# Norm factors computed in four column groups and spread by DMA, in the local layers and in sink attention

## The chip, the cores and the metric

The kernel runs on one core of one Trainium2 chip. The metric is the device time of one execution in microseconds, here the median over runs of the same kernel. A core has a tensor engine (PE, whose weight loads are shown apart as PEld), a vector engine (DVE), a scalar engine (ACT), GpSimd (POOL) and a queue engine (SP) that issues most transfers. They run side by side and wait for each other through semaphores. Operands lie in an on-chip memory of 128 partitions; products land in PSUM, which has eight banks of 128 x 512 fp32.

## The reference

The program is a network of sixteen residual blocks over x of 16 x 256 tokens with 128 channels, all in fp32. Each block computes `x = x + block(layernorm(x))`. Two blocks matter here.

The local block (it occurs twice, each time as two layers one after the other): half of the channels are shifted by one token, then projected to queries, keys and values of 8 heads of 64; these are normalized, rotated, and attended in windows of 64 tokens that see themselves and the window before. After the output projection and a residual sum, half of the channels are shifted again, a layer norm with gain `lg` and bias `lb` follows, and a gated feed-forward part with 341 hidden channels.

The sink-attention block (it occurs once): an RMS norm, grouped attention with 16 query heads and 4 key heads, interleaved rotary positions, a band of 128 tokens, and one sink logit per head:

```
combined = jnp.concatenate([scores, sink], axis=-1)
probs = jax.nn.softmax(combined, axis=-1)[..., :-1]
out = jnp.einsum('buqk,bkuh->bquh', probs, v)
```

The kernel computes in this block both the outer layer norm with its inner RMS norm (two factors from one variance), and after the attention the RMS norm that the mixture of experts starts from (one factor).

What is changed is how one number per token, `1 / sqrt(mean of squares + eps)`, comes about and reaches all 128 partitions.

## The kernel before

Activations lie transposed: channels on partitions, tokens along the free dimension. The 4096 tokens are cut into `NCH = 8` chunks of `CH = 512`, or `NTILE = 32` tiles of `P = 128`. A norm has three steps. `centre_step` multiplies a chunk by `cent` (identity minus 1/128) on PE, which subtracts the mean over channels; ACT copies the result out and POOL (or ACT) squares it into `nsq`. `spread_step` multiplies `nsq` by `mean`, a 128 x 128 matrix filled with 1/128. The product holds the same variance on each of the 128 partitions, so it is summed and spread at once; ACT turns it into the factor `nrs` in two passes over 128 x 512 (Ln with eps added, then Exp scaled by -0.5), or four passes where two factors are wanted. The third step multiplies the chunk by the factor on DVE. Constants (`cent`, `mean`, the identity) lie in the tile `ct`, which is the name that the profile shows.

The stages concerned run under a schedule written out by hand: each engine executes its instructions in the order in which the loops record them.

`local_attend` loops over m from -9 to 37. One step of m scores and weighs one unit of work (a 256-token stretch and half of the heads), turns and rotates one tile of queries and keys, and projects a tile that is needed five steps later. Within a step the order is: scores, weighing, output projection every fourth step, transposes and values (`turn`), exponentials, `rotate`, the inverse of the sums and the division (`rd`, `ot`), `unit`, then `chunk_steps`, then `project`. The norm steps stand in `chunk_steps`: for the first layer of a pair the norm of x of chunk c at m = 4c - 9, 4c - 8, 4c - 7 (chunks 0 to 4 were normalized by the stage before, `led`), and in both layers the norm ahead of the feed-forward part (`norm_of_half`) at m = 4c + 6 to 4c + 9, for chunks 0 to 6. PSUM is shared as three banks `w` (projections, transposes, norms), four `s` (scores) and one `o`.

`window_attention` is the sink attention. It loops over n; each n scores one of 128 units, and each odd n weighs two. Even n carry the rest: `prepare` (the rotary projections of a chunk's half: key and first query group, two groups, one group, none, in four even n one after the other), `out`, `before(c, 0..2)` for the norm before attention of chunk c at n = 16c - 14, -12, -10, and `after(c, 0..2)` for the norm after it at n = 16c + 24, +26, +28. Scores, projections and norms share four `s` banks. A matrix product can only start when the last reader of the bank it gets is done, and which bank it gets is settled when the program is built.

Transfers: weights of a coming stage are loaded on SP by `ahead`, three DMAs each, which wait until the stage that used the buffer is done. During the first local layer, SP also issues 66 transfers (`fill_rooms`) that initialize tables in device memory for the later expert stages: `rows` in 64 transfers of 520 KB and two small ones. No transfer takes part in any norm.

Of the kernel before, what the change touches and what calls it, by code (L numbers as in the profile page):

```python
# [11 lines left out]
F32, BF16, I32 = mybir.dt.float32, mybir.dt.bfloat16, mybir.dt.int32  # L12
SP = mybir.EngineType.SP
AF = mybir.ActivationFunctionType
# [3 lines left out]
P = 128  # L18
B, T, C = 16, 256, 128
NT = B * T  # L20
CH = 512
NCH = NT // CH
# [1627 lines left out]
class Fast(Net):  # L1650
# [120 lines left out]
            self.gt(sq, dst, dst, ALU.mult)  # L1771
        return sq

    def spread_step(self, pool, sq, bank, eps="eps5", twice=False):


        pv = self.bank(bank)
        self.mm(pv, self.k["mean"], sq)
        out = []
        for n in range(2 if twice else 1):  # L1780
            rs = pool.tile([P, CH], F32, tag=f"nrs{n}", name="nrs", bufs=2)
            if n:
                self.act(rs, pv, AF.Ln, scale=1.0 + 1e-5, bias=self.k["eps10"])
            else:
                self.act(rs, pv, AF.Ln, bias=self.k[eps])
            out.append(rs)
        for rs in out:
            self.act(rs, rs, AF.Exp, scale=-0.5)
        return out if twice else out[0]

    def norm_steps(self, pool, src, dst, bank, g=None, b=None, eps="eps5", copy=None, square=False):


        held = {}

        def centre():
            held[0] = self.centre_step(pool, src, dst, bank, copy, square)

        def spread():
            held[1] = self.spread_step(pool, held[0], bank, eps)  # L1800

        def scale():
            if g is None:
                self.tt(dst, dst, held[1], ALU.mult)
            else:
                self.stt(dst, dst, g, held[1], ALU.mult, ALU.mult)
                self.ts(dst, dst, b, ALU.add)

        return [centre, spread, scale]

    def norm_x_step(self, pool, c, i, bank="ps", copy=None):

        if c in self.led:
            return
        if i == 0:
            s = self.chunk(c)
            self.norms[c] = self.norm_steps(pool, self.x[:, s], self.ha[:, s], bank, copy=copy)
        self.norms[c][i]()

    def slots(self, n, *steps, last=(), every=1):  # L1820
# [1339 lines left out]
    def window_attention(self, w, h, n1, ns2):  # L3160


        nc = self.nc
        with ExitStack() as st:
            p1 = self.stage(st, "w1", 1)
# [27 lines left out]
            def later(slot, f, *args):  # L3193
                due.setdefault(slot, []).append((f, args))
# [24 lines left out]
            def score(n):  # L3219
                c, side, b, it, jt = units[n]  # L3220
                i0, j0 = b * T + it * P, b * T + jt * P
                q, k = qs[2 * c + side], ks[2 * c + side]
                pt = p2.tile([P, 2, 4, P], F32, tag="pt", name="pt", bufs=6)
                ps = [self.bank("s"), self.bank("s")]
                for half in range(2):
                    rows = slice(64 * half, 64 * half + 64)
                    self.mm(ps[half].rearrange("p (h t) -> p h t", h=4), k[rows, j0 : j0 + P], q[rows, :, i0 : i0 + P])
                for half in range(2):
                    self.act(pt[:, half].rearrange("p h t -> p (h t)"), ps[half], AF.Exp)
                pts[n] = pt  # L3230
# [53 lines left out]
            def out(i):  # L3284
                c, side = divmod(i, 2)
                pz = self.bank("s")
                ot = ots.pop(i)
                for g in range(4):
                    at = (4 * side + g) * C
                    self.mm(pz, w["Wof"][:, at : at + C], ot[:, g], start=g == 0, stop=g == 3)  # L3290
                hs = h[:, self.chunk(c)]
                if side:
                    self.tt(hs, hs, pz, ALU.add)
                else:
                    self.stt(hs, pz, w["bo"], hs, ALU.add, ALU.add)

            held = {}

            def before(c, i):

                s = self.chunk(c)
                if i == 0:
                    held["sq"] = self.centre_step(p1, self.x[:, s], h[:, s], "s", square=True)
                elif i == 1:
                    held["rs"] = self.spread_step(p1, held["sq"], "s", twice=True)
                else:
                    r1, r2 = held["rs"]
                    self.stt(n1[:, s], h[:, s], w["ns1"], r2, ALU.mult, ALU.mult)
                    self.tt(h[:, s], h[:, s], r1, ALU.mult)

            def after(c, i):

                s = self.chunk(c)
                if i == 0:
                    held["sq"] = p1.tile([P, CH], F32, tag="nsq", name="nsq", bufs=2)
                    self.act(held["sq"], h[:, s], AF.Square)
                elif i == 1:
                    held["rs"] = self.spread_step(p1, held["sq"], "s")
                else:
                    self.stt(n1[:, s], h[:, s], ns2, held["rs"], ALU.mult, ALU.mult)  # L3320

            with self.share(s=4, o=4), self.tc.manual_schedule():
                self.logs()
                for n in range(-14, len(units) + 16):
                    if 0 <= n < len(units):
                        score(n)
                        later(n + 1, masked, n)
                    for f, args in (*due.pop(n, []), *due.pop(("last", n), [])):
                        f(*args)
                    if n % 2:  # L3330
                        for i in (n - 3, n - 2):
                            if 0 <= i < len(units):
                                weigh(i, n)
                        continue
                    i, step = divmod(n + 8, 8)
                    if 0 <= i < 2 * NCH:
                        prepare(i, step // 2, n)
                    i, rest = divmod(n - 14, 8)
                    if rest == 0 and 0 <= i < 2 * NCH:
                        out(i)  # L3340
                    c, u = divmod(n + 14, 16)
                    if u in (0, 2, 4) and c < NCH:
                        before(c, u // 2)
                    c, u = divmod(n - 24, 16)
                    if u in (0, 2, 4) and 0 <= c < NCH:
                        after(c, u // 2)

    def local_begin(self):
        pass
# [8 lines left out]
    def local_attend(self, w, z, hs, last):  # L3358
# [5 lines left out]
        nc = self.nc  # L3364
        with ExitStack() as st:
            p = self.stage(st, "l1", 1)
# [15 lines left out]
            made, rot, qkt, val, weights, sums, outs, steps, spare = {}, {}, {}, {}, {}, {}, {}, {}, []  # L3382
# [141 lines left out]
            def chunk_steps(m):  # L3524

                def due(slot):
                    c, rest = divmod(m - slot, 4)
                    return c if rest == 0 and 0 <= c < NCH else None

                if not last:  # L3530
                    for i in range(3):
                        if (c := due(i - 9)) is not None:
                            self.norm_x_step(p, c, i, "w")
                for slot in (-6, 5):
                    if (c := due(slot)) is not None:
                        self.shift(hs[:, self.chunk(c)], z[:, self.chunk(c)])

                for i in range(4):
                    if (c := due(6 + i)) is not None and c < NCH - 1:
                        if i == 0:  # L3540
                            steps[1] = self.norm_of_half(p, "w", w, hs[:, self.chunk(c)])
                        steps[1][i]()

            with self.share(w=3, s=4, o=1), self.tc.manual_schedule():
                self.logs()
                for m in range(-9, NTILE + 6):
# [4 lines left out]
                    c, rest = divmod(m - 5, 4)  # L3551
# [14 lines left out]
                    if within(m + 5, NTILE):  # L3566
                        project(m + 5)

    def norm_of_half(self, pool, bank, w, s):

        held = {}

        def centre():
            held[0] = self.centre_step(pool, s, s, bank)

        def spread():
            held[1] = self.spread_step(pool, held[0], bank)

        return [
            centre, spread, lambda: self.stt(s, s, w["lg"], held[1], ALU.mult, ALU.mult),  # L3580
            lambda: self.act(s, s, AF.Identity, bias=w["lb"]),
        ]
# [263 lines left out]
```

## Time and profile before

| | us |
|---|---|
| median of 3 runs (range) | 4256.13 (4253.08 to 4257.88) |
| profiled execution, its own time | 4251.58 |
| span of the profiled execution | 4249.8 |
| PE busy, over the span | 3860.8 (91%) |
| DVE busy | 2557.6 (60%) |
| ACT busy | 2327.2 (55%) |
| POOL busy | 1852.0 (44%) |
| `nrs` from PSUM on ACT, 128x512, mean of 208 | 0.683 |
| `nrs` in place on ACT, 128x512, mean of 208 | 0.629 |

Attention of the four local layers runs from about 115, 485, 1125 and 1490 us on, some 280 us each; sink attention runs from about 2915 to 3388 us. The busy time of an engine is the union of its instructions. Line L504 is a matrix product, L508 a transpose, L528 an activation, L531 and L543 are DVE's two- and three-operand operations and L534 is POOL's: they are helpers, so groups are told apart by the names of the tiles. An operand written `ps<-nsq,ct` means that a PSUM tile is written from the tiles nsq and ct. An fp32 product appears as two records, one for each of its two passes.

### The profile page before, as it was taken

The page shows a single profiled execution, that of the slowest core. Times are in us where ns is not written, and L with a number is a line of the kernel's source. Part 1 is how long each engine was busy: PE and PEld are TensorE (multiplying, and loading weights), DVE is VectorE, ACT ScalarE, POOL GpSimd, SP SyncE. Part 2 cuts the span into 40 slices and gives each one's busy share as a digit, 9 for nine tenths or more (in the row PEclk, how much of TensorE's full clock was granted, in tenths as well). Part 3 has the DMA queues.
Part 4 walks back from the last instruction along what each step waited for, and adds up shares of the span by engine and source line. Part 5 has one row for each costly group of instructions (what it writes and reads, how often), then busy time and mean ns, then how long its engine had stood idle before and what let it go on. Part 6 is the DMA issues. An engine that isn't in the chain of part 4 may idle for free. (4 is left out here: it accounts for less than half of the span.)

```text
span 4249.8 us, 73853 instructions
## 1 busy us (share of the span) xinstructions
PE 3860.8 (91%) x28998; PEld 2207.7 (52%) x28998; DVE 2557.6 (60%) x4503; ACT 2327.2 (55%) x4741; POOL 1852.0 (44%) x1632
## 2 busy tenths in 40 slices
PE   7999999998899999995989979888999999899878
PEld 3555466464465456553965459643444344455333
DVE  4775577364477477555336643565788687486474
ACT  6665466554766456553447634444555455774432
POOL 4664365232565166316433334454555455311251
PEclk9999999988999999997999979999999999999989
DMA  1800000000000000002930049100000000000000
GB/s 61 343 1 1 11 1 1 20 1 1 20 1 1 1 4 2 1 1 83 330 125 12 17 137 316 61 19 16 1 1 1 3 1 1 16 2 18 6 0 21
DMA packets 78404, 176.43 MB, mean 42 GB/s; under 512 B 12606, under 2 KB 39108, under 8 KB 77920
## 3 DMA queue, kind: packets, MB, share of 16 engines
q1 hardware_dynamic: 65568, 148.40, 10.1%
q0 software_dynamic: 9120, 18.51, 1.2%
q8 instruction: 231, 3.78, 0.4%
q10 hardware_dynamic: 3360, 4.72, 0.3%
q14 instruction: 125, 1.02, 0.1%
HBM read 118.28 MB, written 54.20 MB: 41 GB/s over the span
## 5 line engine op out<-in xcount | busy, mean ns | idle before, releaser
L528 ACT ACTIVATE pt<-ps 128x512 f32<-128x512 f32 x640 | 340.0, 600 | 327.7 <-PE ps L504 326.4
L504 PE MATMUL ps<-hb,w 128*128 128x512 f32 (+1 forms) x960 | 458.7, 611 | 6.9 <-issue 3.3
L504 PE MATMUL ps<-w,hb 128*128 128x512 f32 (+2 forms) x896 | 403.4, 571 | 27.9 <-DVE t L531 20.9
L534 POOL TENSOR_TENSOR t<-t,t 128x512 f32<-128x512 f32 x256 | 319.3, 1268 | 160.8 <-DVE t L531 101.2
L531 DVE TENSOR_TENSOR t<-ps,tab 128x512 f32<-128x512 f32 x512 | 317.5, 681 | 83.8 <-ACT sq L528 80.3
L534 POOL TENSOR_TENSOR t<-t,ss 128x1024 f32<-128x1024 f32 x128 | 243.5, 1903 | 218.9 <-ACT ss L528 217.6
L504 PEld LDWEIGHTS ps<-hb,w 128*128 128x128 f32 (+1 forms) x960 | 178.0, 190 | 263.7 <-issue 224.3
L528 ACT ACTIVATE qkt<-ps 128x512 f32<-128x512 f32 x256 | 140.5, 595 | 309.0 <-PE ps L508 308.4
L531 DVE TENSOR_TENSOR u<-u,ps 128x384 f32<-128x384 f32 (+1 forms) x206 | 121.8, 595 | 287.9 <-PE ps L508 182.9
L531 DVE TENSOR_TENSOR ot<-ps,rd 128x512 f32<-128x512 f32 (+2 forms) x224 | 143.2, 639 | 232.0 <-ACT rd L528 232.0
L534 POOL TENSOR_TENSOR nsq<-ha 128x512 f32<-128x512 f32 x112 | 122.9, 1097 | 320.4 <-ACT ha L528 308.6
L504 PEld LDWEIGHTS ps<-w,hb 128*128 128x128 f32 x896 | 155.5, 192 | 185.4 <-issue 113.6
L534 POOL TENSOR_TENSOR both<-pt 128x1024 f32<-128x1024 f32 x64 | 151.2, 2362 | 200.0 <-DVE pt L531 164.3
L504 PE MATMUL ps<-nsq,ct 128*128 128x512 f32 x368 | 201.0, 629 | 36.0 <-POOL nsq L534 32.1
L504 PE MATMUL ps<-ot,w 128*128 128x512 f32 x448 | 213.6, 611 | 16.8 <-DVE ot L531 9.0
L504 PE MATMUL ps<-xt,w 128*128 128x128 f32 x1704 | 221.0, 280 | 1.5 <-ACT xt L528 1.5
L2199 POOL DMA_INDIRECT back<-y,x x142 | 138.9, 978 | 184.2 <-ACT y L528 90.4
L504 PE MATMUL ps<-u,w 128*128 128x512 f32 (+1 forms) x448 | 215.4, 605 | 3.4 <-POOL u L534 3.4
L528 ACT ACTIVATE u<-ps,w 128x512 f32<-128x512 f32 x160 | 107.8, 685 | 183.8 <-PE ps L504 181.3
L504 PEld LDWEIGHTS ps<-xt,w 128*128 128x128 f32 x1704 | 204.8, 194 | 2.9 <-ACT xt L528 2.9
L528 ACT ACTIVATE nrs<-ps,ct 128x512 f32<-128x512 f32 x208 | 139.8, 683 | 101.8 <-PE ps L504 95.9
L3743 POOL DMA_INDIRECT rows<-out,idx x128 | 125.8, 982 | 155.1 <-ACT out L528 105.7
(362 smaller groups left out, 8937.9 us busy)
## 6 DMA issues: line engine op xcount, KB each, us to landing
w<-in_moe_x SPq DMA_DIRECT2D x142, 533.0 KB
rows<-t SPq DMA_DIRECT2D x64, 520.0 KB
x<-rows SPq DMA_DIRECT2D x142, 65.0 KB
w<-in_local_f SPq DMA_DIRECT2D x8, 659.5 KB
y<-back ACTq DMA_DIRECT2D x16, 256.0 KB
y<-back SPq DMA_DIRECT2D x16, 256.0 KB
w<-in_local_f SPq DMA_DIRECT2D x4, 658.5 KB
back<-y,x POOLq DMA_INDIRECT x142
```

The source lines that it names most:

```text
L504: self.nc.tensor.matmul(out, lhsT, rhs, start=start, stop=stop)
L528: self.nc.scalar.activation(out, in_, func, **kw)
L531: self.nc.vector.tensor_tensor(out, a, b, op)
L534: self.nc.gpsimd.tensor_tensor(out, a, b, op)
L2199: nc.gpsimd.indirect_dma_start(views[i], bass.IndirectOffsetOnAxis(ap=x[:, C : C + 1].bitcast(I32), axis=0), y, None, bounds_check=2 * NT ...
L3743: nc.gpsimd.indirect_dma_start(views[(c * 2 + k) * 4 + t], bass.IndirectOffsetOnAxis(ap=idx[:, k, t : t + 1], axis=0), out[:, k, t], None,)
```

## The change

A `compact` form of `spread_step` is added. It multiplies the four groups of 128 tokens of a chunk by only 32 columns of `mean`, and puts the result of group r onto partitions 32r to 32r + 31. One PSUM tile of 128 x 128 then holds the variances of all 512 tokens, each on 32 equal rows. ACT's passes run over 128 x 128 elements (two factors: their Exp together over 128 x 256) into a new tile `nrow`. Four DMAs for each factor, issued on SP, write `nrs`: each reads the 32 equal rows of a group four times and fills 128 partitions and 128 columns. The step that scales waits for these DMAs.

The form is used for the norms of x in `local_attend`, for `norm_of_half` on chunks 0 to 6, for the norm before sink attention on chunks 1 to 7, and for the norm after it on chunks 0 to 6. The other norms keep the old form. In sink attention the steps of the loop also move: for chunks 1 to 7, `before` centres and spreads two n earlier (16c - 16 and 16c - 14) and scales at 16c - 10 as it did; `after` scales two n later for chunks 0 to 6 (16c + 30).

```diff
+    def compact_spread(self, pool, sq, bank, eps, twice):
+        nc = self.nc
+        pv = self.bank(bank)
+        for r in range(4):
+            nc.tensor.matmul(
+                pv[32 * r : 32 * r + 32, :P], self.k["mean"][:, :32], sq[:, r * P : r * P + P],
+                start=True, stop=True, skip_group_check=True,
+            )
+        many = 2 if twice else 1
+        rows = pool.tile([P, many, P], F32, tag="nrow", name="nrow", bufs=2)
+        self.act(rows[:, 0], pv[:, :P], AF.Ln, bias=self.k[eps])
+        if twice:
+            self.act(rows[:, 1], pv[:, :P], AF.Ln, scale=1.0 + 1e-5, bias=self.k["eps10"])
+        flat = rows.rearrange("p n t -> p (n t)")
+        self.act(flat, flat, AF.Exp, scale=-0.5)
+        out = []
+        for n in range(many):
+            rs = pool.tile([P, CH], F32, tag=f"nrs{n}", name="nrs", bufs=2)
+            for r in range(4):
+                nc.sync.dma_start(rs[:, r * P : r * P + P], rows[32 * r : 32 * r + 32, n][:, None].broadcast_to([32, 4, P]))
+            out.append(rs)
+        return out if twice else out[0]
...
-                    held["rs"] = self.spread_step(p1, held["sq"], "s", twice=True)
+                    held["rs"] = self.spread_step(p1, held["sq"], "s", twice=True, compact=c > 0)
...
-                    held["rs"] = self.spread_step(p1, held["sq"], "s")
+                    held["rs"] = self.spread_step(p1, held["sq"], "s", compact=c < NCH - 1)
...
-                    c, u = divmod(n + 14, 16)
-                    if u in (0, 2, 4) and c < NCH:
-                        before(c, u // 2)
+                    c, u = divmod(n + 16, 16)
+                    if c == 0 and u in (2, 4, 6):
+                        before(c, u // 2 - 1)
+                    if u in (0, 2, 6) and 0 < c < NCH:
+                        before(c, (u + 1) // 3)
                     c, u = divmod(n - 24, 16)
-                    if u in (0, 2, 4) and 0 <= c < NCH:
-                        after(c, u // 2)
+                    if u in (0, 2, 6 if c < NCH - 1 else 4) and 0 <= c < NCH:
+                        after(c, (u + 1) // 3 + (u == 4))
...
-                            self.norm_x_step(p, c, i, "w")
+                            self.norm_x_step(p, c, i, "w", compact=True)
...
-                        steps[1] = self.norm_of_half(p, "w", w, hs[:, self.chunk(c)])
+                        steps[1] = self.norm_of_half(p, "w", w, hs[:, self.chunk(c)], compact=True)
```

More of the change, by code (lines that the diff above doesn't have):

```diff
@@ L1772, in centre_step, with spread_step @@
         return sq
-    def spread_step(self, pool, sq, bank, eps="eps5", twice=False):
+    def spread_step(self, pool, sq, bank, eps="eps5", twice=False, compact=False):
+        if compact:
+            return self.compact_spread(pool, sq, bank, eps, twice)
         pv = self.bank(bank)
@@ L1789, in spread_step, with norm_steps @@
         return out if twice else out[0]
-    def norm_steps(self, pool, src, dst, bank, g=None, b=None, eps="eps5", copy=None, square=False):
+    def compact_spread(self, pool, sq, bank, eps, twice):
[20 more added lines that the diff above has]
+        return out if twice else out[0]
+    def norm_steps(self, pool, src, dst, bank, g=None, b=None, eps="eps5", copy=None, square=False, compact=False):
         held = {}
@@ L1799, in spread @@
         def spread():
-            held[1] = self.spread_step(pool, held[0], bank, eps)
+            held[1] = self.spread_step(pool, held[0], bank, eps, compact=compact)
         def scale():
@@ L1809, in norm_steps, with norm_x_step @@
         return [centre, spread, scale]
-    def norm_x_step(self, pool, c, i, bank="ps", copy=None):
+    def norm_x_step(self, pool, c, i, bank="ps", copy=None, compact=False):
         if c in self.led:
@@ L1816, in norm_x_step @@
             s = self.chunk(c)
-            self.norms[c] = self.norm_steps(pool, self.x[:, s], self.ha[:, s], bank, copy=copy)
+            self.norms[c] = self.norm_steps(pool, self.x[:, s], self.ha[:, s], bank, copy=copy, compact=compact)
         self.norms[c][i]()
@@ L3567, in local_attend, with norm_of_half @@
                         project(m + 5)
-    def norm_of_half(self, pool, bank, w, s):
+    def norm_of_half(self, pool, bank, w, s, compact=False):
         held = {}
@@ L3576, in spread @@
         def spread():
-            held[1] = self.spread_step(pool, held[0], bank)
+            held[1] = self.spread_step(pool, held[0], bank, compact=compact)
         return [
```

## The prediction

> **What bounds the kernel now.** I read the two-tenths rows of the page for the stages, then busy time by stretch, then the order of instructions inside one step, since the change lives in two stages that a mean over the span hides. Busy time by stretch (first columns: stretch, its us, then PE, PEld, DVE, ACT, POOL busy; then granted clock); a first local layer, a second one, and the sink-attention stage:
>
> ```profile
> 140.00:380.00 240.00, 232.40 (x2310) 144.53 (x2309) 178.09 (x262) 156.68 (x413) 146.97 (x129) 1.00 0.28 111
> 500.00:745.00 245.00, 239.72 (x2468) 151.99 (x2467) 177.49 (x269) 159.35 (x427) 148.22 (x129) 1.00 0.01 2
> ...
> 2940.00:3380.00 440.00, 437.23 (x3428) 179.25 (x3426) 349.56 (x550) 231.44 (x509) 245.37 (x141) 1.00 0.00 1
> ```
>
> PE is busy 97 to 99% at full clock, DVE 73 to 79%, ACT 53 to 65%. A busy PE need not be a full one, so I looked at its instructions in one step of a second local layer (start, us, engine, line, operands; each fp32 product is recorded as two passes):
>
> ```profile
> 593.34 1.02 PE L504 MATMUL ps<-w,hb 128*128 128x512 f32 x2
> ...
> 594.20 1.02 PE L504 MATMUL ps<-nsq,ct 128*128 128x512 f32 x2
> ...
> 595.06 1.88 PE L504 MATMUL ps<-w,hb 128*128 128x512 f32 x4
> ...
> 595.94 0.40 ACT L528 ACTIVATE rd<-ps 128x256 f32<-128x256 f32 x1
> ...
> 596.77 0.39 PE L504 MATMUL ps<-masked,identb 128*128 128x128 bf16 x4
> ```
>
> Starts follow each other every 0.43 us per pass: there is no hole. The spread's product, nsq by ct, holds PE for 595.06 - 594.20 = 0.86 us. So what is worth money is PE time, and only where PE does not then wait for someone else.
>
> **What the Trainium skill says.** "TensorEngine Tiling (Array Packing)", Theoretical Speedup and Key Properties: products with at most 32 stationary columns can run four at once, up to 4 times faster, and a change of tiling mode drains the array. The trace agrees on both, below. "DMA: Bandwidth & Descriptors", Anatomy of one DMA: about 2 us fixed per DMA (fitted for GpSimd's queue); here the final output DMAs show less. The same page, Queues, rings and completion order: an engine consumes descriptors in ring order, so a small DMA behind large ones on SP waits for them; the trace of before has no such pair to show it.
>
> **The change, part by part.** The built program has 48 compact spreads: 10, 7, 10, 7 in the four local layers and 14 in sink attention, 7 of these with two factors. That is 55 factors, so 220 DMAs of 64 KB on SP.
>
> PE. The weighing uses the same form, four 32-column products side by side over 128 columns:
>
> ```profile
> 208.12 0.40 PE L3487 MATMUL ps<-pu,v 128*32 128x128 f32 x8
> ...
> 208.34 0.51 PE L3487 MATMUL ps<-pt,v 128*32 128x192 f32 x8
> ```
> ```profile
> 592.08 0.40 PE L3487 MATMUL ps<-pu,ct 128*32 128x128 f32 x8
> ...
> 592.41 1.09 PE L508 MATMUL ps<-ct,t 128*128 128x128 f32 x8
> ```
>
> A group of four takes 0.22 us (208.34 - 208.12), and 0.33 when a full-array product follows: leaving the mode costs 0.11. Entering it from full mode I take as 0.09, from the change of full to row mode in the sink stage (0.95 below against 0.86). Sum 0.42, saving 0.86 - 0.42 = 0.44 us. Bounds: 0.33 with a free entry (saves 0.53), 0.60 if the entry loses two more passes' setup (saves 0.26).
>
> ACT. Two activations of 128x512 (683 and 629 ns by their groups) become two of 128x128; the nearest row, pu from PSUM, is 279 ns. That gives 0.75 us per spread. ACT is off the path, so nothing, except that squares behind it start sooner.
>
> Where the 0.44 us goes. In second layers it survives only while PE does not overtake ACT: the masks after the projections need the bank that ACT reads as rd, done at 595.94 + 0.40 = 596.34. PE comes at 596.77, so 0.43 us of room plus the first two masks: just covered. Of the 34 local spreads, 6 (chunks 1 to 3 of both first layers) stand in a step where the next norm's centring shares the banks:
>
> ```profile
> 233.14 0.58 ACT L528 ACTIVATE ha<-ps 128x512 f32<-128x512 f32 x1
> ...
> 233.77 1.13 PE L504 MATMUL ps<-w,hb 128*128 128x512 f32 x2 [0.74 <-ACT ha L528]
> ```
>
> PE already waits 0.74 us there for ACT's copy, which does not move: these 6 gain 0. The last compact chunk of each layer stands in the tail, where PE waits on DVE and ACT 0.62 us just after it: 4 gain 0. Left: 24 x 0.44 = 10.6 us.
>
> Sink attention. A spread there costs 0.95 us, and 0.53 is offered. But all 14 now stand behind two rotary projections:
>
> ```profile
> 3023.37 1.98 PE L504 MATMUL ps<-hb,w 128*128 128x512 f32 x4
> ...
> 3025.19 1.02 PE L504 MATMUL ps<-nsq,ct 128*128 128x512 f32 x2
> 3025.20 0.74 DVE L543 SCALAR_TENSOR_TENSOR q<-ps,w 128x512 f32<-128x512 f32 x1
> ...
> 3026.14 1.13 PE L504 MATMUL ps<-q,k 64*128 64x512 f32 x4
> ```
>
> The scores at 3026.14 need four banks' oldest: the first projection's, free when DVE ends at 3025.94. PE ready at 3025.61 would wait. In 7 (before attention) the gain is some 0.15; in the other 7 the built program gives the scores the spread's own bank, free after ACT's logarithm at about 3025.28 + 0.20 + 0.28 + 0.28, so 0.05. Together 1.4 us. Moving the centring two slots ahead takes 0.86 from one step and puts it in another, where DVE frees the first bank at 2991.72 and PE would come at 2991.92: nothing, and up to 0.3 x 7 if that cover is gone. Scaling after attention moves two slots later; nobody in the stage waits for it.
>
> The DMAs. Three loads take 1.29 us to issue, so 0.48 apart. The second output DMA (256 KB) was issued by 4234.22 and released DVE at 4235.65, so 64 KB lands in at most 1.4 us. Four factors: 3 x 0.48 + 1.4 = 2.9 us; eight: 4.8. The consumer comes 7.2 us after the Exp in second layers (564.03 to 571.27), 3.5 in the tail (409.5 to 413.0), and over 13 in sink attention after the move. Hidden, cover lost only beyond 7.2 us (tail 3.5); then DVE stands still with its rotary products queued behind, and PE waits for these. The bytes, 14 MB over some 1400 us, are no load. On SP these DMAs are put behind a wait once: before layer 1's first spread stands the zero-fill.
>
> ```profile
> 111.76 0.33 SPq L2129 DMA_DIRECT2D back<-t  x1
> 113.03 0.82 SPq L2128 DMA_DIRECT2D rows<-t  x2
> 114.99 1.50 SPq L615 DMA_DIRECT2D w<-in_local_f  x3
> 116.53 84.83 SPq L2128 DMA_DIRECT2D rows<-t  x64
> ```
>
> SP is free at 201.36, but the last fill packets run to 208.1, and the consumer wants its factor at 207.4: some 1.5 us late on DVE, I take 1 on PE, once. Weight loads pushed behind the spreads (performer at 480.65 before) waited for their buffer until then anyway: nothing.
>
> Sum: -10.6 - 1.4 + 1.0 = -11.0 us. The profiled execution took 4251.58 us, 4.55 under the median of the runs shown, so 4240.6 on its scale, 4245 on the median's.
>
> **Rivals.** (a) Full saving: everything PE no longer does is gained, 34 x 0.44 + 14 x 0.53 = 22.4 us, 4234. For it: PE busy shares. Against: the bank waits above. (b) It does nothing: entry and exit drains and the ACT cover eat it, -4 us or less, 4252 to 4256. For it: cover of 0.43 against 0.44; against: the drains measured. (c) Slower: the factors land late. If each DMA of a factor began only when the one before had landed, four would take 4 x (0.48 + 1.4) = 7.5 us or, at the skill's 2 us, 9.9, beyond the 7.2 from which it decides; the in-order DVE would lose up to 2.7 us in each of 24 spreads that PE feels, less 11: up to +50, likelier some +15, 4271. Against: three loads issued 0.48 apart without waiting for each other.
>
> **How the numbers follow.** My sum 0.60, (a) 0.16, (b) 0.13, (c) 0.11. The likeliest case alone spans 4238 to 4250 (24 x 0.26 to 0.53, first stall 0 to 2 us). The range reaches over (a) and most of (b): 4233 to 4256. A change under 0.2% (8.5 us) can hardly be told from none here; a part of my own case falls inside it, and (b) does: faster 0.71, same 0.18, slower 0.11.
>
> **What would show it.** nsq by ct at 128x128 in groups 0.42 us before the next product; PE busy in the local stretches down by 0.44 us per spread but a wait of some 0.3 us on DVE or ACT before the scores after each spread in sink attention; the wait on ACT's ha copy grown from 0.74 to about 1.2; factors landing about 3 us after the Exp; DVE idle on a DMA once, near 207. Chunk pitch 34.35 to about 33.9 us in second layers, 56.65 to about 56.4 in sink attention. Wrong if DVE's scaling rows show DMA waits in every chunk, or if the pitch in sink attention falls by a whole 1 us.

## The result, and the profile after

The changed kernel takes 4249.18 us (median of 15 runs, 4243.12 to 4250.94) where the kernel before takes 4256.13 us in the same comparison (15 runs, 4251.52 to 4260.14): a ratio of 0.9983, 95% interval 0.9975 to 0.9991. That is 6.95 us, or between 3.8 and 10.6. The gain is real and lies just inside the 0.2% bound that the prediction set for "can hardly be told from none". The forecast was 4245, its range 4233 to 4256.

The profiled execution took 4250.35 us, with a span of 4248.6. This is only 1.2 us less than the span before, so the two traces can't be compared end to end. Between them lie differences in stages that the change doesn't touch: 1.66 us before the first local layer has even begun its windows, 3.4 us where the expert stage waits for its first gathered rows, and dips of PE's granted clock that cost some 1.6 us each and fall elsewhere in each execution (the 30 us behind the last tile of the first local layer had 0.94 of the full clock in the trace of before and 1.00 in this one). I therefore compare stage by stage: for one VectorE instruction that occurs once per tile in the local layers (the reduction of squares, `ss<-sq`) and one per chunk in sink attention (the sum into `ha`), the starts in the two traces give the length of each chunk. Undisturbed chunks agree within 0.02 us from run to run, so a tenth of a microsecond can be read.

| stretch | before | after | difference |
|---|---|---|---|
| first local layer, chunk with the first spread | 34.13 | 37.66 | +3.53 |
| first layers, chunk with two spreads | 37.95 | 37.38 | -0.57 |
| second layers, chunk with one spread | 34.35 | 33.70 to 33.76 | -0.65 to -0.59 |
| sink attention, chunk | 56.65 | 56.61 | -0.04 |
| sink attention and its run-in, 2823 to 3384 us of before | 560.5 | 559.8 | -0.7 |

Nineteen chunks of the local layers became shorter by 0.56 to 0.65 us, one of them by only 0.31, together 11.0 us. One more became 3.5 us longer. With sink attention the sum is -11.0 + 3.5 - 0.7 = -8.2 us, inside the interval of the measurement.

Busy time by stretch of the changed kernel, for the three stretches shown in the prediction (columns: stretch, its us, then PE, PEld, DVE, ACT and POOL busy; then granted clock, DMA share, GB/s):

```profile
140.00:380.00 240.00, 229.47 (x2366) 143.15 (x2365) 175.53 (x260) 150.49 (x409) 146.11 (x127) 0.99 0.33 122
...
500.00:745.00 245.00, 239.84 (x2508) 152.26 (x2508) 178.02 (x270) 156.35 (x429) 148.63 (x129) 0.99 0.03 8
...
2940.00:3380.00 440.00, 436.91 (x3515) 180.25 (x3512) 348.75 (x549) 218.36 (x499) 245.38 (x141) 1.00 0.06 14
```

ACT lost 13 us in sink attention and PE's busy share hardly moved: in a fixed window, shorter work is followed at once by more work. In the first stretch PE idles 10.5 us where it idled 7.6. That is the stall below. Busy shares alone would have told almost nothing here.

One step of a second local layer, in order of time, the step that the prediction showed at 593 to 597:

```profile
593.09 1.02 PE L504 MATMUL ps<-w,hb 128*128 128x512 f32 x2
...
594.04 0.42 PE L1798 MATMUL ps<-nsq,ct 128*32 128x128 f32 x8
...
594.39 1.98 PE L504 MATMUL ps<-w,hb 128*128 128x512 f32 x4
...
596.22 0.39 PE L504 MATMUL ps<-masked,identb 128*128 128x128 bf16 x4
...
596.79 0.35 ACT L528 ACTIVATE nrow<-ps,ct 128x128 f32<-128x128 f32 x1
...
597.17 0.31 ACT L528 ACTIVATE nrow<-nrow 128x128 f32<-128x128 f32 x1
```

The four products with eight passes take 594.39 - 594.04 = 0.36 us (by the unrounded starts). The product ahead of them occupies PE 0.52 us in place of 0.43, which is the entry into the mode. Over both, PE spends 0.88 us where it spent 1.29: it saves 0.41. ACT's two instructions take 0.35 and 0.31 us in place of 0.67 and 0.63: it saves 0.64.

The first spread of the first local layer, the same view:

```profile
198.66 5.25 SPq L2154 DMA_DIRECT2D rows<-t  x4
...
200.82 0.31 ACT L528 ACTIVATE nrow<-nrow 128x128 f32<-128x128 f32 x1
...
205.05 4.66 SPq L1813 DMA_DIRECT2D nrs<-nrow  x4
...
214.60 0.75 DVE L543 SCALAR_TENSOR_TENSOR hb<-hb,w,nrs 128x512 f32<-128x512 f32 x1 [6.14 <-DMA nrs<-nrow]
...
216.61 2.31 PE L508 MATMUL ps<-ct,t 128*128 128x128 f32 x8 [2.36 <-DVE t L531]
```

The factor is ready at 201.13. SP still issues the zero-fill until 203.91, and then takes 4.66 us for four DMAs that take 2.5 elsewhere. The issues themselves are no slower (0.54 to 0.67 us each): SP waits between them. What it waited for (us in total, times, longest; four of the five waits are of these DMAs):

```profile
SPq L1813 <- DMA rows<-t: 4.4, 5, 1.1
```

By the semaphores in the trace, each of the four goes out only when the transfer issued eight before it has landed. For the first, at 205.05, that is a fill transfer issued at 192.85, which landed at 204.98. The last goes out at 209.17 and lands at 214.48. DVE stands still for 6.14 us, and PE, which needs DVE's rotary products, for 2.36 there and some more in the next steps: 3.53 in all.

A spread in sink attention, that of the norm after attention, the same view:

```profile
3022.98 0.43 PE L1798 MATMUL ps<-nsq,ct 128*32 128x128 f32 x8
...
3023.34 1.68 PE L504 MATMUL ps<-q,k 64*128 64x512 f32 x4
3023.48 0.37 ACT L528 ACTIVATE nrow<-ps,ct 128x128 f32<-128x128 f32 x1 [0.20 <-PE ps L1798]
...
3023.89 0.29 PEld L504 LDWEIGHTS ps<-q,k 64*128 64x128 f32 x2 [0.26 <-ACT nrow L528]
...
3024.95 1.45 PEld L3283 LDWEIGHTS ps<-pt,v 128*32 128x32 f32 x32 [0.76 <-issue]
```

The score products after the spread take 3024.95 - 3023.34 = 1.61 us. Before, with the same four passes, they took 1.06. They are two products of 64 rows each, which normally run side by side on the two halves of the array: in the trace of before they start at 3026.138 and 3026.145. Here the first starts at 3023.34 and its partner only at 3023.90. The partner gets the spread's own bank, and ACT's logarithm reads that until 3023.48 + 0.37 = 3023.85. The pair is broken and costs 0.55 us, where the spread itself saves 0.95 - 0.36 less 0.09 for the entry, 0.50.

The chunk's other spread, that of the norm before attention:

```profile
3052.57 0.74 DVE L543 SCALAR_TENSOR_TENSOR q<-ps,w 128x512 f32<-128x512 f32 x1
...
3053.00 1.54 PE L504 MATMUL ps<-q,k 64*128 64x512 f32 x4
...
3054.48 1.45 PEld L3283 LDWEIGHTS ps<-pt,v 128*32 128x32 f32 x32 [0.76 <-issue]
```

Here the partner's bank is the first projection's, which DVE reads until 3052.57 + 0.74 = 3053.31. The partner starts 0.45 us after the first, and the scores take 1.47 us (by the unrounded starts), 0.41 more than usual. Per chunk 2 x 0.50 - 0.55 - 0.41 = 0.04 us is left.

### The profile page after: what moved, and what is told of

It reads as the page before. It is cut to its first block, busy times and chain, and to the rows that moved or that the text cites. A ratio compares the mean times of both kernels' runs of the same rounds, so it can differ in the third digit from the quotient of the medians.

```text
span 4248.6 us, 74911 instructions
## 1 busy us (share of the span) xinstructions
PE 3851.9 (91%) x29286; PEld 2206.0 (52%) x29286; DVE 2556.4 (60%) x4503; ACT 2294.4 (54%) x4734; POOL 1851.8 (44%) x1632
## 3 DMA queue, kind: packets, MB, share of 16 engines
q14 instruction: 129, 1.06, 0.1%
## 5 line engine op out<-in xcount | busy, mean ns | idle before, releaser
L504 PE MATMUL ps<-ha,w 128*128 128x512 f32 x320 | 174.9, 668 | 14.9 <-ACT f L528 6.8
L504 PE MATMUL ps<-nsq,ct 128*128 128x512 f32 x272 | 154.5, 652 | 33.7 <-POOL nsq L534 29.7
```

Of the source, the lines that this page charges most:

```text
L504: self.nc.tensor.matmul(out, lhsT, rhs, start=start, stop=stop)
```

## The experiments

The experiments ran in three groups, each on one chip and each with the kernel before beside it. The chips differ (before took 4256.8, 4273.5 and 4255.0 us on the three), so between groups only ratios and chunk lengths are set side by side.

**The two places apart.** `local_only` keeps the compact spread in the local layers, with the sink attention of before; `sink_only` the reverse.

```diff
 # local_only
-held["rs"] = self.spread_step(p1, held["sq"], "s", twice=True, compact=c > 0)
+held["rs"] = self.spread_step(p1, held["sq"], "s", twice=True)
-held["rs"] = self.spread_step(p1, held["sq"], "s", compact=c < NCH - 1)
+held["rs"] = self.spread_step(p1, held["sq"], "s")
 # and the slots of before(c, i) and after(c, i) as they were
 # sink_only
-self.norm_x_step(p, c, i, "w", compact=True)
+self.norm_x_step(p, c, i, "w")
-steps[1] = self.norm_of_half(p, "w", w, hs[:, self.chunk(c)], compact=True)
+steps[1] = self.norm_of_half(p, "w", w, hs[:, self.chunk(c)])
```

> The compact spread stays in the four local layers; the sink-attention stage is that of before. My theory after reading the two traces: nearly all of the gain is in the local layers (about 0.58 us per chunk, less 3.5 us of one stall behind the zero-fill and about 0.5 us in each tail), so some 6 us stay: 4250 us, ratio 0.9985. Rival: the sink attention gives as much as its 14 spreads offer (14 x 0.5 = 7 us) and the local layers give nearly nothing after their stall: 4254 to 4256.

> The compact spread and the moved slots stay in sink attention alone; the local layers are those of before. My theory: the pitch of a chunk in sink attention is 56.61 us against 56.65, so about 1 us in all: 4255 us, ratio 0.9998, and the second score product after each spread waits about 0.5 us. Rival (the sink attention carries the gain): 4249 to 4251.

Measured: `local_only` 4249.22 us, ratio 0.9979 (0.9971 to 0.9987); `sink_only` 4256.71 us, ratio 1.0002 (0.9994 to 1.0010). The chunk lengths are those of the changed kernel in the part that is kept (33.71 to 33.78 and 56.60) and those of before in the other (34.35, 56.64). The whole gain is in the local layers. The change in sink attention, 14 of the 48 spreads and all the moved slots, gives nothing that a time can show.

**The stall.** `first_full` makes only the very first spread in full, so that no DMA has to pass the zero-fill. `first_full2` is the same kernel again.

```diff
+            self.settled = self.filled
             self.fill_rooms(st)
...
-  steps[1] = self.norm_of_half(p, "w", w, hs[:, self.chunk(c)], compact=True)
+  steps[1] = self.norm_of_half(p, "w", w, hs[:, self.chunk(c)], compact=c > 0 or self.settled)
```

> Only the first spread of the first local layer, the one whose four DMAs stand behind the zero-fill, is made in full again; all others stay compact. My theory: the 6.1 us wait of VectorE and the 2.4 us of TensorE near 214 us go, and nothing takes their place: some 3.2 us less than the changed kernel, 4246 us. Rival 1: the zero-fill still reaches the next spread's DMAs at 237 us, and a wait of 1 us or more moves there: 4248 to 4249. Rival 2: the loss in this layer is not the DMA's: no change, 4249.

> The same kernel as first_full, timed once more. It took 4236.9 us where its trace shows 3.5 us taken off the stall near 214 us; the other 8.7 us against the changed kernel lie in stages that the edit does not touch (the gather of the experts, ends of layers). If those are chance of five runs, this one gives 4244 to 4247 us; if they belong to the kernel, 4236 to 4238 again.

Measured: 4236.93 us, ratio 0.9954 (0.9941 to 0.9967), and the second time, on another chip, 4261.74 us, ratio 0.9972 (0.9960 to 0.9984). VectorE's part of the trace of `first_full`, at the place of the stall:

```profile
206.30 0.69 DVE L531 TENSOR_TENSOR ot<-ps,rd 128x512 f32<-128x512 f32 x1 [0.96 <-ACT rd L528]
206.91 2.30 DVE L543 SCALAR_TENSOR_TENSOR hb<-hb,w,nrs 128x512 f32<-128x512 f32 x1
```

The scaling follows the division without a wait, and the chunk is back at 34.13 us (34.12 in the repeat), as before: 3.53 us gained, and the next spreads wait for nothing. So the mechanism holds. Against the changed kernel's ratio the first group's times gave 12 us, the second's some 5. In the first, 3.4 us of the surplus are the expert stage's wait for its gathered rows, which the changed kernel's trace has and that of `first_full` has not; the rest is not explained. What the traces attribute to the edit is 3.5 us.

**ScalarE's share.** The chunks of second layers shrank by 0.59 us, PE's own saving is 0.41. `act_long` lets ACT work as long as before, with PE still compact.

```diff
+ wide = pool.tile([P, 4, P], F32, tag="nrw", name="nrw", bufs=2)
+ self.act(wide, pv[:, :P][:, None].broadcast_to([P, 4, P]), AF.Ln, bias=self.k[eps])
+ self.act(wide, wide, AF.Exp, scale=-0.5)
 # and the four DMAs read one of the four equal copies
```

> The changed kernel with ScalarE's logarithm and Exp of each single factor made over 128x512 again (the 128 columns read four times, one copy used), so that ScalarE works as long as before while TensorE keeps the compact product. Theory: the chunk of a second local layer gained 0.59 us where TensorE's own part is 0.41 (1.29 to 0.88 us from the product before to the product after), and the rest came from ScalarE being done earlier before the copies of pu that TensorE waits for: the pitch goes from 33.76 to about 33.93 us. Rival: ScalarE is off the path as predicted, and the rest has another source: 33.76 stays.

Measured: one execution, 4254.65 us, and the chunk of the second layers is 34.34 to 34.40 us, not 33.93: the whole gain is gone, not a third of it. In the first layers 38.01 in place of 37.38. The reason is visible in one step. The kernel before (this and the next two fences: the order of time, the step after a spread in the second local layer):

```profile
599.24 0.45 ACT L528 ACTIVATE pu<-ps 128x128 f32<-128x128 f32 x2
...
599.74 0.16 PEld L3487 LDWEIGHTS ps<-pt,ct 128*32 128x32 f32 x8 [0.33 <-ACT pu L528]
599.74 0.53 PE L3487 MATMUL ps<-pt,ct 128*32 128x192 f32 x8
```

The changed kernel:

```profile
598.34 0.45 ACT L528 ACTIVATE pu<-ps 128x128 f32<-128x128 f32 x2
...
598.94 0.51 PE L3515 MATMUL ps<-pt,ct 128*32 128x192 f32 x8
```

`act_long`:

```profile
597.88 0.67 ACT L528 ACTIVATE nrw<-ps,ct 128x512 f32<-128x512 f32 x1
...
598.59 0.63 ACT L528 ACTIVATE nrw<-nrw 128x512 f32<-128x512 f32 x1
...
600.08 0.44 ACT L528 ACTIVATE pu<-ps 128x128 f32<-128x128 f32 x2
...
600.58 0.53 PE L3523 MATMUL ps<-pt,ct 128*32 128x192 f32 x8 [0.35 <-ACT pu L528]
```

PE weighs with `pt` and `ct` only after ACT has copied `pu`, and ACT comes to this copy only after Ln, Exp and the two squares. Before, PE already waited here, by 0.24 us (0.46 from start to start in place of 0.22). In `act_long`, PE arrives 0.41 earlier, ACT doesn't, and PE waits 0.54 (0.76 from start to start). In the changed kernel ACT is 0.64 earlier and the wait is gone. So ACT's shorter passes are worth all of the 0.59: with PE's saving alone the chunk gains nothing. With ACT's alone (not run) at most the 0.24 of the wait could go.

**Whether the landing is hidden.** `dma_x3` issues every factor DMA three times; `dma_act` issues them on ACT's queue.

```diff
 # dma_x3
+for again in range(3):
     nc.sync.dma_start(rs[:, r * P : r * P + P], rows[32 * r : 32 * r + 32, n][:, None].broadcast_to([32, 4, P]))
 # dma_act
-nc.sync.dma_start(
+nc.scalar.dma_start(
```

> The changed kernel with each factor DMA issued three times, the same bytes to the same place. Theory: SP issues one per 0.64 us, so twelve take 7.0 us and land about 9 us after the Exp, past the 7.2 us of cover in the second local layers; VectorE waits about 2 us in each chunk there, TensorE feels most of it, and the pitch goes from 33.76 to 35 us or more; in sink attention eight factors become 24 issues, 15.4 us against 13 of cover, and the pitch grows too. Rival: the DMAs overlap or VectorE's queue absorbs the wait, and the pitch stays under 34.2 us.

> The changed kernel with the factors' DMAs issued by ScalarE, behind its own Exp, in place of SP. Theory: of the 9 us between the first spread's Exp at 201.1 and its landing near 214, 3.9 us were SP still issuing the zero-fill (its first factor DMA came at 205.05); these go, VectorE's wait falls from 6.1 to about 2 us and TensorE's 2.4 us to nothing: 4246 us. Rival 1: the bytes of the zero-fill ahead on the DMA engines decide, the wait stays near 6 us: 4249. Rival 2: the issuing occupies ScalarE some 0.6 us per DMA, 2.4 us per spread, and delays the exponentials that TensorE waits for: in every chunk 1 us or more, 4280 or above.

`dma_x3` took 4864.79 us in its one execution, its chunk in the first second local layer 46.0 to 46.3 us and in sink attention 85 to 91. The direction is that of the theory, the size is not: I had taken the copies to overlap, but SP issued the second and third copy to a place only when the one before had landed, 2.1 us after its issue (issues at 693.82, 695.94 and 698.01 for one place; copies to different places follow each other in 0.6 us). VectorE and PE behind these copies, in the same layer:

```profile
700.22 0.75 DVE L543 SCALAR_TENSOR_TENSOR hb<-hb,w,nrs 128x512 f32<-128x512 f32 x1 [13.57 <-DMA nrs<-nrow]
```
```profile
702.23 2.31 PE L508 MATMUL ps<-ct,t 128*128 128x128 f32 x8 [9.79 <-DVE t L531]
```

DVE stands idle for 13.6 us in a chunk that became 12.3 us longer. So when the cover is exceeded in every chunk, nine tenths of what a factor is late is paid by the chunk; at the single stall behind the zero-fill it was 3.5 of 6.1 us. This is the price that the prediction's rival (c) named; it doesn't test where its limit of 7.2 us lies.

`dma_act` took 4376.33 us, ratio 1.0249 (1.0227 to 1.0270): rival 2. A step of a second local layer in its trace:

```profile
581.98 2.51 ACTq L1813 DMA_DIRECT2D nrs<-nrow  x4
...
584.54 1.08 ACT L528 ACTIVATE sq<-ps 128x512 f32<-128x512 f32 x2 [2.59 <-DMA nrs<-nrow]
...
585.51 0.46 ACT L528 ACTIVATE pu<-ps 128x128 f32<-128x128 f32 x2
586.02 0.16 PEld L3515 LDWEIGHTS ps<-pt,ct 128*32 128x32 f32 x8 [2.69 <-ACT pu L528]
586.02 0.53 PE L3515 MATMUL ps<-pt,ct 128*32 128x192 f32 x8 [2.42 <-ACT pu L528]
```

Four DMAs keep ACT from its next instruction for 2.59 us, and PE waits 2.42 us at the very place that `act_long` names; a chunk is 3.4 us longer (185.73 - 168.69 over five). This agrees with the Trainium skill, "Perfetto Trace Analysis", What "DMA-bound" means: the slice on the issuing engine's sequencer is the making of descriptors, not the movement of data. On SP nobody stands behind it; on ACT the softmax does. At the zero-fill, VectorE's scaling in this kernel came at 212.0 without a wait. Its first factor had landed at 206.15, 5.8 us after the Exp, where the changed kernel needs 13.3 there and 4.2 without traffic. But SP had issued no fill from 196.7 to 202.6, since its fill waited for these very DMAs, so this run doesn't separate SP's order from the bytes ahead. The changed kernel's own trace does in part: from the Exp to the last of the four issues 8.0 us pass there in place of 1.9, and from this issue to the landing 5.3 in place of 2.2. SP's waiting for fill transfers is thus 6.1 of the 9.1 us that traffic added, the slower landing the rest.

**Sink attention without the broken pair.** If the loss there is the pair of score products, another order should bring back 0.5 us per spread. `spread_ahead` issues the norm's step ahead of the two rotary projections in the same slot. `own_slot` puts the spreads into the two slots of a chunk that hold no rotary projection, and `own_slot2` also puts the centring back to its slot, one chunk earlier.

```diff
 # spread_ahead: the block with before(c, i) and after(c, i) stands ahead of prepare and out
 # own_slot, own_slot2: ahead of prepare and out
+ c, u = divmod(n + 16 + 2, 16)
+ if u == 0 and 0 < c < NCH:
+     before(c, 1)
+ c, u = divmod(n - 24 - 14, 16)
+ if u == 0 and 0 <= c < NCH - 1:
+     after(c, 1)
 # behind them: before(c, 2) at n = 16c - 14, after(c, 0) and (c, 2) at n = 16c + 34 and 16c + 42
 # own_slot:  before(c, 0) at n = 16c - 20
 # own_slot2: before(c, 0) at n = 16c - 32 (chunk 1: -4), with a dictionary of its own
```

> In sink attention the norm's step of a slot is issued ahead of the two rotary projections, not behind them, so that the score products behind take the spread's own bank and an older one, and not the first projection's. My theory (the compact spread's 0.5 us is lost because the pair of score products is broken while VectorE frees the first projection's bank): the pitch falls from 56.61 to about 55.7 us, some 6 us in all, 4243 us. Rival: another limit lies just behind (VectorE is busy 79% of this stage; another bank's wait), the pitch stays above 56.3 us: 4247 to 4249.

> In sink attention the compact spreads move into the two slots of a chunk that hold no rotary projection, and go ahead of the output projection there; the other two steps of each norm move along. The score products behind the spread then need banks that ScalarE has read long before. My theory (the 0.5 us of a compact spread is lost to a broken pair of score products, whichever bank is late): the pitch falls from 56.61 to about 55.7 us, some 6 us in all, 4243 us. Rival (VectorE or ScalarE bound just behind PE): the pitch stays above 56.3 us.

> own_slot with the norm's centring back in the slot where the changed kernel has it, one chunk earlier (in own_slot it stood behind a projection and the values, and the score products behind it took 2.39 us where 1.06 is usual). Theory: the spreads keep their 0.36 us with no broken pair behind, the 1.33 us go, and the pitch falls from 56.61 to about 55.65 us; some 6 us less than the changed kernel. Rival: another wait comes up, 56.3 us or more.

`spread_ahead`: 4253.66 us, ratio 0.9992 (0.9984 to 1.0000), chunk 56.8 us. Nothing gained. The theory had named only VectorE's bank; in the norm after attention it was the spread's own already in the changed kernel. The norm before attention in the trace of `spread_ahead`:

```profile
3053.51 0.63 ACT L528 ACTIVATE rd<-ps,es 128x128 f32<-128x128 f32 x2
...
3054.18 0.42 ACT L528 ACTIVATE rd<-rd 128x256 f32<-128x256 f32 x1
3054.50 0.62 ACT L528 ACTIVATE nrow<-ps,ct 128x128 f32<-128x128 f32 x2
...
3054.65 1.65 PE L504 MATMUL ps<-q,k 64*128 64x512 f32 x4
```

Now this pair too waits for the spread's own bank. I had said that ACT frees it early; but ACT was behind with `rd` and reads it until 3054.50 + 0.62. The pair is broken again, with 1.58 us to the next product: another engine, a like loss. In the norm after attention the scores took 1.30 us, less than in the changed kernel, but the pair behind the moved centring, which now needs a bank that ACT reads, took 0.39 more.

`own_slot`: 4270.21 us, ratio 0.9988 (0.9979 to 0.9997), chunk 56.98 us, worse still, but for a reason that confirms the cause:

```profile
3154.45 1.12 PE L504 MATMUL ps<-hb,w 128*128 128x512 f32 x2
...
3155.41 1.03 PE L504 MATMUL ps<-w,hb 128*128 128x256 f32 x4
...
3156.28 1.02 PE L504 MATMUL ps<-x,ct 128*128 128x512 f32 x2
...
3157.23 1.12 PE L504 MATMUL ps<-q,k 64*128 64x512 f32 x2
...
3158.59 1.09 PE L504 MATMUL ps<-q,k 64*128 64x512 f32 x2 [0.24 <-DVE q L543]
```

The scores behind both spreads took their usual 1.06 us. But the centring (`x` by `ct`) now stood behind a projection and the values, the scores behind it needed the projection's bank, which DVE read until 3157.72 + 0.73, and took 2.39 us, with the partner starting 1.36 us late. Moved back in `own_slot2`, this goes, and in its trace the spread is followed by the output projection and then by an unbroken pair:

```profile
3119.15 0.42 PE L1798 MATMUL ps<-nsq,ct 128*32 128x128 f32 x8
...
3119.51 3.70 PE L504 MATMUL ps<-ot,w 128*128 128x512 f32 x8
3123.14 1.13 PE L504 MATMUL ps<-q,k 64*128 64x512 f32 x4
...
3124.20 1.93 PE L3283 MATMUL ps<-pt,v 128*32 128x256 f32 x32
```

The chunk is 55.64 us, 0.97 less than in the changed kernel, as expected; the time is 4241.32 us, ratio 0.9966 (0.9952 to 0.9979). About 3.8 us of it stay in this stage (556.0 in place of 559.8 from run-in to end), since the run-in became longer by some 4 us (143.5 and 35.9 us for its two parts in place of 140.9 and 34.6), for a reason that stays open. `act_long` had already shown, unintended, that the bank decides: its build gives the scores of the norm after attention the other bank, they take 1.47 us in place of 1.61, and its chunk in sink attention is 56.47 us, although ACT's passes are longer there.

**The best of them.** `best2` joins `own_slot` with `first_full` and full spreads at the end of each attention; `best3` joins `own_slot2` with `first_full`.

> own_slot together with three full spreads in the place of compact ones: the first local layer's first, and the last one inside the attention of each local layer. Theory: first_full's gain of 3.5 us (or of 12 us, if that repeats) and own_slot's 6 us add up: 4240 us (4231). The full spread at the end of the attentions is worth nothing or 0.4 us less each. Rival: sink attention does not gain, 4245 (4237).

> own_slot2 together with the full first spread of first_full. Theory: 3.5 us and about 6 us add up, so some 9 to 10 us less than the changed kernel, ratio to the kernel before 0.9960 (0.9945 to 0.9972). Rival: sink attention does not gain and only first_full's share stays, 0.9972.

`best2`: 4264.59 us, ratio 0.9979 (0.9972 to 0.9986), its rival's case, as `own_slot` itself gained nothing. `best3`: 4233.27 us (4227.59 to 4234.98), ratio 0.9946 (0.9932 to 0.9959), with chunks of 34.13, 33.7 and 55.64 us. It beats both kernels: 0.54% under the kernel before, where the change alone is 0.17%. Of the some 16 us by which this lies under the changed kernel, the traces attribute 3.5 to the first spread and 3.8 to sink attention; the rest falls in stages that these edits don't touch.

## Why the prediction was right, and where it was not

**The local spreads, -10.6 us: right in size, wrong in why.** PE's saving per spread was put at 0.44 and is 0.41; the entry was put at 0.09 and is 0.09. The forecast was 24 spreads of 0.44; measured are 19 chunks of 0.58 on average, 11.0 us. The step that failed is "ACT is off the path, so nothing". I had looked at the two masks behind the spread and found PE's room just covered, and had not followed ACT's queue on to the copies of `pu`, where PE already waited 0.24 us. `act_long` shows that without ACT's shorter passes the local layers gain nothing. My rival (b), that ACT's cover eats the gain, was thus nearer to the truth than the case that I chose; it failed only because the same edit took 0.64 us from ACT. The two sizes came out alike by luck: fewer places gained than I had counted, and each gained more.

**The six spreads beside `ha`, 0: right.** A chunk with two spreads gains 0.57 us, one with a single spread 0.59, so the one beside `ha` adds nothing. PE's wait there grew by 0.30 us; the forecast was 0.46.

**The tail, 0: right, and more of it.** Two spreads per layer, not one, stand where nothing is gained: in second layers five of seven count. A factor lands 4.2 us after its Exp there, not 2.9. Changed kernel, end of the first local layer's attention:

```profile
410.42 0.31 ACT L528 ACTIVATE nrow<-nrow 128x128 f32<-128x128 f32 x1
410.76 2.49 SPq L1813 DMA_DIRECT2D nrs<-nrow  x4
...
414.91 0.75 DVE L543 SCALAR_TENSOR_TENSOR hb<-hb,w,nrs 128x512 f32<-128x512 f32 x1 [0.53 <-DMA nrs<-nrow]
```

Issues are 0.64 us apart where 0.48 was taken from weight loads, and a factor's DMA lands 2.1 us after its issue (median of the 220), not 1.4. The 1.4 was misread: what ended VectorE's wait at 4235.65 in the trace of before was the first of the two output DMAs, issued at 4233.13; the second landed at 4236.78, 2.6 us after its issue. The 2 us that the prediction set aside was the better figure. The cover of 3.5 us is exceeded by 0.5 us in three layers and by 1.7 in the fourth. I found no loss from it on PE: with a full spread there, in `best2`, the stretches from the attention's end to the next layer are as in `first_full2` within 0.2 us.

**Sink attention, -1.4 us: the mechanism right, the size half.** The scores do wait for the two banks that were named, each in its seven spreads. A pair of scores was to lose 0.38 us behind the norm before attention and 0.48 behind the one after; it lost 0.41 and 0.55. The saving was to be 0.53 and is 0.50. Each is a small miss, but the forecast gain of 0.15 and 0.05 was the difference of the two, and what is left of it is 0.09 and -0.05. The pitch became 56.61, not 56.4; the stage gained 0.7 us. That the moved slots cost nothing holds.

**The first spread behind the zero-fill, +1.0 us: the place and the chain right, the term mis-sized.** It is 3.5 us. SP's time was nearly right: it was done with the fill at 203.9 in a trace that runs 1.7 us late, so 202.2 against the forecast 201.4. What failed is "the last fill packets run to 208.1, some 1.5 us late on DVE". In the trace of before, fill packets run on to 210.7, and in the changed kernel to 213.1; the factor landed 1.4 us after them, at 214.5, and DVE had waited for it 6.1 us. So the landing does follow the fill, as the prediction had it, but the fill's end was read too early. The Trainium skill's statement that was leaned on ("DMA: Bandwidth & Descriptors", Queues, rings and completion order) is that each DMA engine takes descriptors in the order of its ring; this trace agrees, since the last factor packets end at 213.9, behind the last of the fill. It adds that SP itself held its issues back until earlier fill transfers had landed, and that all this makes 13.3 us from Exp to landing, against 4.2 without traffic.

Summed: -10.6 came out as -11.0, -1.4 as -0.7, +1.0 as +3.5. The forecast of -11.0 became -8.2 by the traces, and -6.95 (3.8 to 10.6) by the times. Rival (a) falls with the bank waits that were named against it. Rival (c) falls for the changed kernel, since only the first spread of all is late enough to matter; `dma_x3` shows that its price, nearly all of the lateness, was right where every chunk is late. The span of 4238 to 4250 given for the likeliest case mixes the two scales: its lower end, 24 x 0.53 without a stall, is 4238 on the profiled execution's and 4242 on the median's.

## What to carry to other kernels

When an edit shortens work on two engines, price it on both: follow the other engine's queue from the edited instruction to the next thing that the bound engine waits for, even if that engine is busy only 65% of the time. A small DMA in a per-step loop is free where a queue is idle and its landing has cover, but look for the one place where a bulk transfer is in front of it, and keep the old form there. And if products run in pairs on parts of the array, the head start of one is worth nothing: what the other's bank is late is lost in full. So move the short product to a slot where the next pair's banks were read long ago.

## What the runs showed of the hardware that I had not expected

Issuing a DMA from ACT's queue keeps ACT from its next instruction for about 0.65 us each (2.59 us for four), about as long as the issue is shown on SP. Behind 520 KB transfers SP started its four small DMAs 1.3 to 1.4 us apart in place of 0.64; the issues took no longer, but each waited for an earlier large transfer to land. And a pair of products on the two halves of the array loses what its second one starts late, though the first is already running: 0.25 us late cost 0.24 (`spread_ahead`), 0.45 cost 0.41 and 0.56 cost 0.55 (the changed kernel), and 1.36 cost 1.33 (`own_slot`).
